# A third buffer for the odd slots' tiles, logits turned one group at a time, and a small product moved into its neighbour's PSUM pair

## The chip, the cores and the metric

The kernel runs as one program on 1 core of one Trainium2 chip. The metric is the device time of the program in microseconds, as the median of several runs. All data are 32-bit floats.

## The reference, cut to what matters

Two layers are applied to x of shape (2, 512, 32, 32). The first is an attention with deformable sampling and a learned position bias, followed by a two-matrix MLP; the second is a plain attention over the 1024 pixels. What the change touches is in the first:

```python
q = _gconv1x1(xn, qw)                        # 8 groups of 64 channels, 2 images: 16 (image, group) pairs
off = ...                                    # strided depthwise conv of q, gelu, 1x1, tanh: 64 sampled places a group
kv = _grid_sample(xn, vgrid_scaled)          # 64 sampled columns for each group
k = _gconv1x1(kv, kw); v = _gconv1x1(kv, vw)
pos = grid_q[:, :, None, :] - grid_kv[:, None, :, :]          # 1024 queries x 64 keys x 2
bias = jnp.sign(pos) * jnp.log1p(jnp.abs(pos))
bias = jax.nn.relu(bias @ cpb_w1 + cpb_b1)                    # 2 -> 128
bias = jax.nn.relu(bias @ cpb_w2 + cpb_b2)                    # 128 -> 128
bias = (bias @ cpb_w3 + cpb_b3)                               # 128 -> 1
sim = jnp.einsum('bhid,bhjd->bhij', qh, kh) + bias
attn = jax.nn.softmax(sim, axis=-1)
out = jnp.einsum('bhij,bhjd->bhid', attn, vh)
```

The bias is a small network of 128 hidden units evaluated at 16 x 1024 x 64 points. It is most of the kernel's work.

## The kernel before, in words

**The main loop** (`for s in range(NS)`, 256 slots) evaluates the bias network. There are 16 groups (image b, channel block k, half f), each with 16 slots; a slot takes 4 of the group's 64 keys and all 1024 queries. In each slot:

- `st_layer1` (L616, on VectorE, DVE): one custom instruction adds the x part and the y part of the first layer for 4 keys and clips at 0. It fills a tile h of 128 x 4096. There are 3 such tiles (tag h1), so DVE can be at most some two slots ahead of TensorE (PE).
- `st_layer2` (L633, on PE): for z = 0 to 3, eight matmuls of 128 x 32 weights by 512 columns fill a PSUM pair (two banks, 128 x 1024). Four of them work side by side on the four groups of 32 columns of the array. The pairs come from a pool `zp` of 3, which everything else that `flat(...)` asks for also draws on. ScalarE (ACT) evicts each pair with a relu: z = 0 and 2 into `rx` (3 tiles; L642), z = 1 into `ua`, `uo` or `uc` by the slot's number (L644), z = 3 into `ub` (L644). Odd slots use `uo`, of which there are 2; so a place is used again four slots later.
- `st_sum` (L652, DVE): rx and its mate are summed with weights, in place in the u tile. For z = 2 a DMA on GpSimd's queue (L654) then adds `ub` to the u tile.
- `st_fold`, `st_join`, `st_fold2`, `st_join2` (L671, L678, L687): the u tiles of eight slots are folded into one by accumulating DMAs on POOL's queue and copying DMAs on SP's queue. These read the `uo` tiles, and an eviction into `uo` has to wait for them.
- every eighth slot `st_layer3` (L719): four matmuls with the third layer's weights for each of two halves of the slots, into the group's PSUM tile `sim`, on four column groups; at the start of a pair of groups, four matmuls of q and k (L702) are put in `sim` first.

**The background.** `later()` is a generator advanced once a slot. For each channel block it makes the convolution, the offsets and the sampling; in `sample` the sampled columns kv are multiplied (L485) by the keys' weights into a pair `pkk`, of which 64 columns are used, and (L487) by the values' folded weights into a pair `pkv`, of which the first 256 columns of each bank are used. ACT then copies both out (L491, L493). kv itself comes from an addition on DVE (L478).

**The softmax.** `softmax_steps(gi)` is a generator for each group, advanced in three slots of four, one group after the other. It copies `sim` into half of a tile `ss` (L733). For f = 0 it then ends, but for the last pair. For f = 1 it transposes both halves, 8 times 128 x 128 (L744) into a pair `pt`; ACT copies it as 128 x 1024 into `sx` (L746); DVE finds the maxima (L751, L752); ACT takes exponentials (L757) and scales them (L766). At the end eight transposes (L775) write the attention back through `pb`.

**The order.** The instructions are recorded in the order of the loop; a scheduler then orders each engine's stream by what it expects to be ready, within the bounds that `issue_after` sets. So an edit in one place can move neighbours in another. [...]

**After the loop** come the output projection (L903), the MLP (L956) and the second layer (L1087, L1185), in which matrix products are made with seven block products instead of eight.

Of the kernel before, what the change touches and what calls it, by code (L numbers as in the profile page):

```python
# [8 lines left out]
F32 = mybir.dt.float32  # L9
AF = mybir.ActivationFunctionType  # L10
# [4 lines left out]
P = 128  # L15
# [3 lines left out]
DH = 64  # L19
J = 64  # L20
# [26 lines left out]
def conv_seq_kernel(ctx: ExitStack, tc: tile.TileContext, x, xt, kst, pst, cst, vec, wsm, outw, w1, w2, wl, wlt, brow, out):  # L47
    nc = tc.nc
# [6 lines left out]
    ident = cp.tile([P, P], F32, name="ident")  # L55
# [4 lines left out]
    def col(name, i=0):  # L60
        return vs[:, VOFF[name] + i : VOFF[name] + i + 1]
# [17 lines left out]
    ub = cp.tile([P, 2, NCH], F32, name="ub")  # L79
# [3 lines left out]
    kz = cp.tile([P, NCH * B, J], F32, name="kz")  # L83

    f_pool = ctx.enter_context(tc.tile_pool(name="fp", bufs=1))
    vp = f_pool.tile([P, NCH * B, C], F32, tag="vp", name="vp")
    sx = f_pool.tile([P, 8, 2, J], F32, tag="sx", name="sx")
# [47 lines left out]
    def flat(name):  # L135
        return zp.tile([P, 2, 512], F32, tag="ps2", name=name).rearrange("p h n -> p (h n)")
# [4 lines left out]
    with tc.tile_pool(name="lp", bufs=2) as lp:  # L141
# [51 lines left out]
        uo = vp[:, NCH : 2 * NCH, :]  # L193
# [221 lines left out]
        def sample(ci):  # L415
            G = CHAINS[ci]
            K = len(G)
            th = state[ci]
            gx = th[:, 0:2].rearrange("p i g j -> p (i g j)")

            nc.vector.tensor_scalar(gx, gx, 1.0, 16.0, ALU.add, ALU.mult)
            if ci > 0:
                yield


            sg = ph.tile([P, 5, 2, K * J], F32, tag="fe", name="sg")
            hat = sg[:, 0:4].rearrange("p a f j -> p (a f j)")[:, 0 : 4 * K * J]
            nc.scalar.activation(hat, gx, AF.Abs, bias=edge[:, 0:1])
            nc.scalar.activation(hat, hat, AF.Relu, bias=edge[:, 1:2])
            nc.scalar.activation(hat, hat, AF.Relu, bias=1.0, scale=-1.0)  # L430
            yield
            nc.vector.tensor_tensor(sg[:, 4], sg[:, 0], sg[:, 1], ALU.mult)
            hx = ph.tile([P, 2, K, J], F32, tag="hx", name="hx")
            hxf = hx.rearrange("p f k j -> p (f k j)")
            nc.scalar.activation(hxf, th[:, 0].rearrange("p g j -> p (g j)"), AF.Abs, bias=hb[:, 0:1])
            nc.scalar.activation(hxf, hxf, AF.Relu, bias=1.0, scale=-1.0)
            yield
            gy = th[:, 1].rearrange("p (f k) j -> p f k j", f=2)
            for i, (b, k) in enumerate(G):
                g = b * NCH + k  # L440
                xnt = ph.tile([P, 8, P], F32, name="xnt")
                nc.sync.dma_start(out=xnt, in_=xt[:, b, k])
                wk = ph.tile([P, P], F32, name="wk")
                nc.sync.dma_start(out=wk, in_=wsm[:, 512 + k * P : 512 + k * P + P])
                wt = ph.tile([P, 8, 2, J], F32, tag="xn", name="wt")
                for t in range(8):
                    if t == 4:
                        yield
                    nc.scalar.activation(wt[:, t], gy[:, :, i, :], AF.Abs, bias=hb[:, 1 + t : 2 + t])
                yield  # L450
                wtf = wt.rearrange("p t f j -> p (t f j)")
                nc.scalar.activation(wtf, wtf, AF.Relu, bias=1.0, scale=-1.0)

                kv, uv = (ph.tile([P, J], F32, name=name) for name in ("kv", "uv"))
                rowwise, natural = "p (e i t) -> p e i t", "p (i e t) -> p e i t"
                for f in range(2):
                    r, v = slice(64 * f, 64 * f + 64), sg[:, 4, f, i * J : (i + 1) * J]
                    nc.scalar.activation(
                        uv[r].rearrange(rowwise, e=2, t=16), v[r].rearrange(natural, e=2, t=16), AF.Copy,
                        scale=col("bn1b", k)[r],  # L460
                    )
                yield
                nc.vector.tensor_tensor(
                    wt, wt, hx[:, :, i, :].unsqueeze(1).to_broadcast([P, 8, 2, J]), ALU.mult
                )
                yield
                ps = flat("pkv")
                for t in range(8):
                    for f in range(2):
                        r = slice(64 * f, 64 * f + 64)  # L470
                        nc.tensor.matmul(
                            ps[r, 0:J], xnt[:, t, r], wt[:, t, f, :], start=(t == 0), stop=(t == 7)
                        )
                nc.scalar.activation(
                    kv.rearrange(rowwise, e=2, t=16), ps[:, 0:J].rearrange(natural, e=2, t=16), AF.Copy,
                    scale=bns[:, k : k + 1],
                )
                nc.vector.tensor_tensor(kv, kv, uv, ALU.add)  # L478
                if i + 1 == K and ci + 1 < len(CHAINS):
                    xn0.append(load(*CHAINS[ci + 1][0]))  # L480
                yield


                ps, pk = flat("pkv"), flat("pkk")
                nc.tensor.matmul(pk[:, 0:J], wk, kv, start=True, stop=True)  # L485
                for f_, h_, f, h in QUADS:
                    nc.tensor.matmul(  # L487
                        ps[h_, f * 512 : f * 512 + 256], kv[f_, :], uo[f_, k, h * 256 : (h + 1) * 256],
                        start=True, stop=True,
                    )  # L490
                nc.scalar.activation(kz[:, g], pk[:, 0:J], AF.Copy, scale=DH ** (-0.5))  # L491
                for f_, h_, f, h in QUADS:
                    nc.scalar.copy(vp[f_, g, h * 256 : (h + 1) * 256], ps[h_, f * 512 : f * 512 + 256])  # L493
                yield
            state[ci] = None
# [52 lines left out]
        head, g, n = chain(0), weights(0), weights(1)  # L548
# [24 lines left out]


        NS = NG * NSL
        tabs, h1s, sums, sims, logits, added = {}, {}, {}, {}, {}, {}
        evicted, raw = {}, {}


# [46 lines left out]
        def st_layer2(s):  # L626
            h1 = h1s.pop(s)
            r = []
            for z in range(4):
                ps = zp.tile([P, 2, 512], F32, name="ps2")  # L630
                for h in range(2):
                    for q in range(4):
                        nc.tensor.matmul(  # L633
                            ps[32 * q : 32 * q + 32, h, :], cw2[:, 32 * z : 32 * z + 32],
                            h1[:, 16 * h : 16 * h + 16, q, :], start=True, stop=True,
                        )
                name, bufs = (
                    ("rx", 3), (("ua", 4), ("uo", 2), ("uc", 2), ("uo", 2))[s % 4], ("rx", 3), ("ub", 3)
                )[z]
                o = lp.tile([P, 2, 512], F32, name=name, bufs=bufs)  # L640
                if z % 2 == 0:
                    nc.scalar.activation(o, ps, AF.Relu, bias=sc[:, 4 + z : 5 + z])  # L642
                else:
                    nc.scalar.activation(o, ps, AF.Relu, bias=sc[:, 4 + z : 5 + z], scale=sc[:, z : z + 1])  # L644
                r.append(o)
                if z % 2 == 1:
                    evicted.setdefault(s, []).append(nc.cur_bb.bb.instructions[-1])
            sums[s] = r
# [78 lines left out]
        def softmax_steps(gi):  # L727
            b, k, f = groups[gi]
            sim = sims.pop(gi)
            if f == 0:  # L730
                logits[0] = f_pool.tile([P, 2, 512], F32, name="ss")
            ss = logits[0]
            nc.scalar.activation(ss[:, f], sim, AF.Identity, bias=col("cb3"))  # L733
            yield

            of = [f] if gi >= NG - 2 else [0, 1][: 2 * f]
            if not of:
                return
            n = len(of)
            pt = flat("pt")  # L740
            for i, g in enumerate(of):
                for c in range(4):
                    o = 512 * i + c * P
                    nc.tensor.transpose(pt[:, o : o + P], ss[:, g, c * P : (c + 1) * P], ident)  # L744
            e = sx[:, :, of[0] : of[-1] + 1, :]
            nc.scalar.copy(  # L746
                e.rearrange("p a f j -> p f a j"), pt[:, 0 : 512 * n].rearrange("p (f a j) -> p f a j", f=n, j=J)
            )
            yield
            mx = f_pool.tile([P, 8, 2], F32, name="mx", bufs=2)  # L750
            nc.vector.tensor_reduce(mx[:, :, 0:n], e, AX.X, ALU.max)  # L751
# [20 lines left out]
            for h in range(2):  # L772
                for c in range(4):
                    n = h * 512 + c * P
# [13 lines left out]
        for s in range(NS):  # L788
# [12 lines left out]
            if s + 2 < NS:  # L801
                st_layer1(s + 2)
            st_layer2(s)


# [18 lines left out]
            if bg is None and s > ready and (s - ready) % 4 == 0 and (s - ready) // 4 <= 8:  # L824
                i = (s - ready) // 4 - 1
# [32 lines left out]
    uc = xq.tile([P, 2], F32, name="uc")  # L858
# [16 lines left out]
    with ExitStack() as top, tc.tile_pool(name="wp", bufs=2) as wp:  # L875
# [13 lines left out]
        for i, (b, h) in enumerate(halves):  # L889
            for o in range(NCH):  # L890
                n = slice(h * 512, (h + 1) * 512)
# [155 lines left out]
        for i, (b, p) in enumerate(units):  # L1047

            j, k = divmod(i, NCH)
# [323 lines left out]
```

## Time and profile before

| what | value |
|---|---|
| median of 3 runs | 2662.8 us (2661.68 to 2663.64) |
| the profiled execution: its own time | 2660.99 us |
| its span | 2659.2 us |
| PE busy | 2633.2 us, 99% |
| DVE busy | 2241.3 us, 84% |
| ACT busy | 1687.2 us, 63% |
| one h of DVE (L616) | 4.40 us |
| one eviction of ACT (L642 and L644) | 1.11 and 1.21 us |
| one sum of DVE (L652) | 1.28 us |

The main loop runs from about 37 to 1911 us. The busy time of an engine is the union of its instructions. A matmul of 512 columns leaves two records in the trace, each modelled as 0.59 us long, and four of them start together on the four column groups every 0.43 us; so "x8" in the timeline can be four matmuls of the program. In an entry of the timeline, the bracket at the end gives how long the engine had been idle and what released it. The releaser is inferred: where several things are waited for, the last to come by the profile is named, and where the engine named had long been done, it was another, often a DMA.

### The profile page before, as it was taken

The numbers are of one execution on the slowest core, as the hardware profiler recorded it, in microseconds if no ns is written. First come the engines' busy times: TensorE is split into PE (matmuls) and PEld (weight loads), VectorE is DVE, ScalarE is ACT, GpSimd is POOL, SyncE is SP. The second block draws the span as 40 slices with busy tenths as digits, with TensorE's granted clock in tenths as the row PEclk, the third lists the DMA queues.
The fourth block names the chain that finished last, engine by engine and source line by source line (L and its number), as shares of the span: only waits on it lengthen the run. The fifth ranks groups of instructions, "written<-read, shape, count | busy, mean of one in ns | idle before, by whom it ended". The sixth has DMA issues, their size and how long they took to land.

```text
span 2659.2 us, 46896 instructions
## 1 busy us (share of the span) xinstructions
PE 2633.2 (99%) x19344; PEld 965.0 (36%) x19344; DVE 2241.3 (84%) x1329; ACT 1687.2 (63%) x2201; POOL 792.3 (30%) x867
## 2 busy tenths in 40 slices
PE   9999999999999999999999999999999999999999
PEld 3332322433333333233323323333334444446454
DVE  7999999999999999999999999999674483466354
ACT  5887898789978888877777777777621131114041
POOL 1333333333333333333333333333343232000000
PEclk9999999999999999999999999999999999999999
DMA  5887878888788887888888888878730111000000
GB/s 187 181 176 169 191 164 171 181 189 180 171 176 174 192 175 172 171 177 176 171 172 183 175 178 178 172 173 181 191 110 33 48 48 48 0 16 0 32 0 32
DMA packets 116293, 366.77 MB, mean 138 GB/s; under 512 B 23376, under 2 KB 27616, under 8 KB 113392
## 3 DMA queue, kind: packets, MB, share of 16 engines
q0 software_dynamic: 69408, 235.31, 46.9%
q1 hardware_dynamic: 46240, 128.15, 13.8%
q8 instruction: 153, 2.51, 0.4%
q14 instruction: 60, 0.49, 0.1%
q10 hardware_dynamic: 432, 0.31, 0.0%
HBM read 74.81 MB, written 6.55 MB: 31 GB/s over the span
## 4 chain that ended last, share of the span: by engine, by line
PE 60%; DMA 25%; DVE 7%; issue 6%; ACT 1%; POOL 1%; SPq 0%; POOLq 0%; DVEq 0%; ACTq 0%
PE ps L633 31%; PE sw L956 14%; PE sw L1087 9%; DMA uc<-uo 7%; DMA uc<-uc 6%; DMA ua<-uc 4%; DMA uc<-ub 4%; DVE h L616 3%; PE sw L1185 2%; DMA ua<-uo 1%; DVE ub L652 1%; PE psg L535 1%; DMA ua<-ua 1%; PE sim L719 1%; DVE uo L652 1%
## 5 line engine op out<-in xcount | busy, mean ns | idle before, releaser
L633 PE MATMUL ps<-h,cw 128*32 128x512 f32 x16384 | 1782.8, 592 | 8.1 <-ACT rx L642 6.1
L616 DVE CUSTOM_DVE_ANT_1 h<-ta,tb 128x4096 f32<-128x4096 f32 (+1 forms) x257 | 1131.0, 4402 | 28.1 <-PE ps L633 24.2
L633 PEld LDWEIGHTS ps<-h,cw 128*32 128x32 f32 x16384 | 554.7, 110 | 1205.0 <-issue 1114.6
L642 ACT ACTIVATE rx<-ps,sc 128x1024 f32<-128x1024 f32 x512 | 568.1, 1110 | 146.3 <-PE ps L633 116.4
L644 ACT ACTIVATE ub<-ps,sc 128x1024 f32<-128x1024 f32 x256 | 308.2, 1204 | 80.5 <-PE ps L633 80.2
L652 DVE SCALAR_TENSOR_TENSOR ub<-rx,sc,ub 128x1024 f32<-128x1024 f32 x256 | 326.8, 1277 | 6.6 <-ACT ub L644 6.6
L671 POOL DMA_DIRECT2D ua<-uc x126 | 158.3, 1272 | 299.5 <-DMA ua<-uc 292.5
L671 POOL DMA_DIRECT2D ua<-ua x189 | 225.4, 1336 | 20.2 <-DMA ua<-uo 16.2
L644 ACT ACTIVATE uo<-ps,sc 128x1024 f32<-128x1024 f32 x128 | 154.2, 1205 | 74.3 <-PE ps L633 46.2
L956 PE MATMUL sw<-xb,w1t 128*128 128x512 f32 x448 | 193.7, 592 | 2.7 <-DVE xs L123 2.7
L956 PE MATMUL sw<-hm,w2t 128*128 128x512 f32 x448 | 193.6, 592 | 0.0
L654 POOL DMA_DIRECT2D uo<-ub x127 | 126.8, 998 | 210.8 <-DVE ub L652 200.1
L652 DVE SCALAR_TENSOR_TENSOR uo<-rx,sc,uo 128x1024 f32<-128x1024 f32 x128 | 163.5, 1278 | 18.9 <-ACT uo L644 18.9
L123 DVE TENSOR_TENSOR hm<-hm,sw 128x1024 f32<-128x1024 f32 x56 | 67.6, 1218 | 104.5 <-PE sw L956 104.3
L671 POOL DMA_DIRECT2D uc<-uo x63 | 54.0, 857 | 340.8 <-DMA uc<-uo 340.4
L956 PEld LDWEIGHTS sw<-xb,w1t 128*128 128x128 f32 x448 | 85.0, 190 | 110.2 <-issue 105.7
L965 ACT ACTIVATE hm<-hm,vs 128x512 f32<-128x512 f32 x64 | 42.6, 713 | 128.4 <-DVE hm L123 128.4
L956 PEld LDWEIGHTS sw<-hm,w2t 128*128 128x128 f32 x448 | 85.1, 190 | 107.1 <-issue 106.2
L123 DVE TENSOR_TENSOR xs<-xs,sw 128x1024 f32<-128x1024 f32 (+1 forms) x48 | 55.6, 1171 | 75.9 <-PE sw L1087 36.0
L654 POOL DMA_DIRECT2D ua<-ub x64 | 59.3, 926 | 178.4 <-DVE ub L652 163.4
L1087 PE MATMUL sw<-aT,vt 128*128 128x512 f32 x224 | 96.7, 593 | 0.3 <-ACT aT L1167 0.3
L596 ACT ACTIVATE ta<-fb,vs 128x512 f32<-128x512 f32 (+1 forms) x65 | 88.5, 1364 | 10.1 <-DMA fb<-fdr 10.1
(247 smaller groups left out, 2191.6 us busy)
## 6 DMA issues: line engine op xcount, KB each, us to landing
uo<-ub POOLq DMA_DIRECT2D x127, 512.0 KB, 5.5
fb<-fdr SPq DMA_DIRECT2D x64, 512.0 KB, 5.2
ua<-ub POOLq DMA_DIRECT2D x64, 512.0 KB, 6.0
uc<-ub POOLq DMA_DIRECT2D x64, 512.0 KB, 5.0
ua<-ua POOLq DMA_DIRECT2D x63, 256.0 KB, 6.3
ua<-uo SPq DMA_DIRECT2D x63, 256.0 KB, 2.5
ua<-uo POOLq DMA_DIRECT2D x63, 256.0 KB, 5.6
uc<-uc POOLq DMA_DIRECT2D x63, 256.0 KB, 7.2
```

The costliest lines, as they stand in the source:

```text
L123: nc.vector.tensor_tensor(out, a, b_, op)
L596: nc.scalar.activation(ta.rearrange("p j x -> p x j")[:, :, j0:j1], fb[:, 0, :, j0:j1], AF.Identity, bias=col("cb1"), scale=col("w1x"),)
L616: nc.vector._custom_dve(TENSOR_ADD_SAT, out=h1[:, y : y + step].rearrange("p y t x -> p (y t x)"), in0=a.unsqueeze(1).to_broadcast([P, ste ...
L633: nc.tensor.matmul(ps[32 * q : 32 * q + 32, h, :], cw2[:, 32 * z : 32 * z + 32], h1[:, 16 * h : 16 * h + 16, q, :], start=True, stop=True,)
L642: nc.scalar.activation(o, ps, AF.Relu, bias=sc[:, 4 + z : 5 + z])
L644: nc.scalar.activation(o, ps, AF.Relu, bias=sc[:, 4 + z : 5 + z], scale=sc[:, z : z + 1])
L652: nc.vector.scalar_tensor_tensor(r[1], r[0], sc[:, z : z + 1], r[1], ALU.mult, ALU.add)
L654: nc.gpsimd.dma_start(out=sums[s][1], in_=sums[s][3], accum_op=ALU.add)
L671: nc.gpsimd.dma_start(out=out, in_=in_, accum_op=ALU.add)
L956: nc.tensor.matmul(ps[:, m, :], w[:, a, k, m * P : (m + 1) * P], x[:, b_, k, :], start=(k == 0), stop=(k == 1),)
L1087: nc.tensor.matmul(ps[:, m, :], w[:, a, k, c + m * P : c + (m + 1) * P], x[b_][:, k, :], start=(k == 0), stop=(k == nk - 1),)
L1185: nc.tensor.matmul(v[:, m, :], xbl[b_][:, k, m * P : (m + 1) * P], gn[:, a, k, :], start=(k == 0), stop=(k == 1),)
```

## The change

Three edits, in one diff:

- `uo` has 3 places instead of 2; a place is used again six slots later.
- `ss` is one tile of 128 x 512 for each group in turn. Each group is transposed in its own step, 4 times 128 x 128 into the first half of a pair `pt`, and ACT copies 128 x 512 into that group's half of `sx`. The rest of the softmax still runs once for both groups of a pair.
- the keys' product goes into columns 256 to 319 of the first bank of the pair that the values' product also uses; `pkk` is gone.

```diff
-                ps, pk = flat("pkv"), flat("pkk")
-                nc.tensor.matmul(pk[:, 0:J], wk, kv, start=True, stop=True)
+                ps = flat("pkv")
+                pk = ps[:, 256 : 256 + J]
+                nc.tensor.matmul(pk, wk, kv, start=True, stop=True)
                 for f_, h_, f, h in QUADS:
...
-                nc.scalar.activation(kz[:, g], pk[:, 0:J], AF.Copy, scale=DH ** (-0.5))
+                nc.scalar.activation(kz[:, g], pk, AF.Copy, scale=DH ** (-0.5))
...
                 name, bufs = (
-                    ("rx", 3), (("ua", 4), ("uo", 2), ("uc", 2), ("uo", 2))[s % 4], ("rx", 3), ("ub", 3)
+                    ("rx", 3), (("ua", 4), ("uo", 3), ("uc", 2), ("uo", 3))[s % 4], ("rx", 3), ("ub", 3)
                 )[z]
...
             sim = sims.pop(gi)
-            if f == 0:
-                logits[0] = f_pool.tile([P, 2, 512], F32, name="ss")
-            ss = logits[0]
-            nc.scalar.activation(ss[:, f], sim, AF.Identity, bias=col("cb3"))
+
+            ss = f_pool.tile([P, 512], F32, name="ss")
+            nc.scalar.activation(ss, sim, AF.Identity, bias=col("cb3"))
             yield
-
+            pt = flat("pt")[:, 0:512]
+            for c in range(4):
+                nc.tensor.transpose(pt[:, c * P : (c + 1) * P], ss[:, c * P : (c + 1) * P], ident)
+            nc.scalar.copy(sx[:, :, f, :], pt.rearrange("p (a j) -> p a j", j=J))
             of = [f] if gi >= NG - 2 else [0, 1][: 2 * f]
             if not of:
                 return
             n = len(of)
-            pt = flat("pt")
-            for i, g in enumerate(of):
-                for c in range(4):
-                    o = 512 * i + c * P
-                    nc.tensor.transpose(pt[:, o : o + P], ss[:, g, c * P : (c + 1) * P], ident)
             e = sx[:, :, of[0] : of[-1] + 1, :]
-            nc.scalar.copy(
-                e.rearrange("p a f j -> p f a j"), pt[:, 0 : 512 * n].rearrange("p (f a j) -> p f a j", f=n, j=J)
-            )
             yield
```

More of the change, by code (lines that the diff above doesn't have):

```diff
@@ L575, in conv_seq_kernel @@
         NS = NG * NSL
-        tabs, h1s, sums, sims, logits, added = {}, {}, {}, {}, {}, {}
+        tabs, h1s, sums, sims, added = {}, {}, {}, {}, {}
         evicted, raw = {}, {}
```

## The prediction, written before the changed kernel was run

> **What bounds the kernel now.** I read the page first, then the table by stages, then the waits, then the timeline of TensorE around each place that the diff touches.
>
> From the page:
> ```profile
> PE 2633.2 (99%) x19344; PEld 965.0 (36%) x19344; DVE 2241.3 (84%) x1329; ACT 1687.2 (63%) x2201; POOL 792.3 (30%) x867
> L633 PE MATMUL ps<-h,cw 128*32 128x512 f32 x16384 | 1782.8, 592 | 8.1 <-ACT rx L642 6.1
> ```
> TensorE is busy 99% of the span: whatever doesn't change its matmul stream or its stalls is worth nothing. The stages (columns: length, then busy time of PE, PEld, DVE, ACT, POOL):
> ```profile
> 620.00:880.00 260.00, 257.33 (x2432) 81.41 (x2424) 259.70 (x139) 223.00 (x316) 93.56 (x108) 1.00 0.80 174
> 921.00:1148.00 227.00, 223.54 (x2098) 68.59 (x2094) 226.23 (x122) 193.37 (x268) 80.93 (x93) 1.00 0.82 175
> 1148.00:1860.00 712.00, 711.46 (x6610) 229.14 (x6606) 690.11 (x318) 540.17 (x636) 260.20 (x299) 1.00 0.82 176
> ```
> The first two rows have DVE at 99.9% and 99.7% while PE stalls: there DVE sets the pace, and PE time saved inside becomes waiting. In the third PE is never idle, so each extra matmul counts. At 541 to 620 and 880 to 921 the timeline shows DVE's h (L616) waiting for PE with its three h tiles full: PE sets the pace.
>
> The waits (us, times, longest), of PE and then of ACT:
> ```profile
> PE ps L633 <- ACT rx L642: 6.1, 11, 1.1
> PE ps L633 <- ACT uo L644: 1.6, 2, 1.5
> ...
> ACT uo L644 <- DMA ua<-uo: 11.8, 8, 2.1
> ACT uo L644 <- DMA uc<-uo: 10.9, 8, 2.9
> ```
> ACT often stands before the eviction into uo until the DMAs that read its old contents are done (22.7 us), but little of it reaches PE. The timeline gives the cases in which it does:
> ```profile
> 256.97 1.21 ACT L644 ACTIVATE uo<-ps,sc 128x1024 f32<-128x1024 f32 x1 [2.88 <-PE ps L633]
> 258.23 2.35 PE L633 MATMUL ps<-h,cw 128*32 128x512 f32 x20 [1.46 <-ACT uo L644]
> ```
> ACT is idle 2.88 us with PE's pair long written; PE, its three pairs full, stops for 1.46 us. The profile names PE as releaser, but PE had gone on and finished: it is the buffer.
>
> The matmuls of the logits (sim), and the transposes:
> ```profile
> 112.33 0.62 PE L719 MATMUL sim<-ua,w3f 128*32 128x512 f32 x1
> 112.78 0.62 PE L633 MATMUL ps<-h,cw 128*32 128x512 f32 x2
> 112.78 0.59 PE L719 MATMUL sim<-ua,w3f 128*32 128x512 f32 x1
> 112.79 14.32 PE L633 MATMUL ps<-h,cw 128*32 128x512 f32 x126
> 127.04 1.09 PE L273 MATMUL psq<-xn,wq 64*64 64x512 f32 x8
> ...
> 1018.94 1.04 PE L719 MATMUL sim<-ua,w3f 128*32 128x512 f32 x8
> 1019.80 0.61 PE L633 MATMUL ps<-h,cw 128*32 128x512 f32 x4
> ```
> ```profile
> 1270.85 1.09 PE L744 MATMUL pt<-ident,ss 128*128 128x128 f32 x8
> 1271.87 2.35 PE L633 MATMUL ps<-h,cw 128*32 128x512 f32 x20
> ...
> 1868.66 0.66 PE L744 MATMUL pt<-ident,ss 128*128 128x128 f32 x4
> 1869.25 2.34 PE L633 MATMUL ps<-h,cw 128*32 128x512 f32 x18
> ```
> [...] Four sim matmuls on the four column groups cost 1019.80 - 1018.94 = 0.86 us together; a single one, behind the keys' product, also keeps its group for 0.86 us.
>
> [...] four records of L633 start together every 0.43 us, and a change of form costs about 0.12 us. [...] ACT stood idle 2.88 us with nothing passed ahead. [...] the small product's eviction (kz) now waits for the last matmul of the pair. [...] the trace has 577 and 1003 for the copies out of pt.
>
> **The change part by part.** The order in which the built program issues the instructions shows, beside the edits, one thing that the diff doesn't: seven times a sim matmul stood alone after the keys' product (six from ua, one from qa), three followed later; now all four stand together at the later place. POOL and SP keep their order; DVE swaps a few neighbours.
>
> 1. Third uo place. It removes waits of at most 2.9 us, one use further back (two slots, some 14 us) being ample. PE stalls that end with it (idle + 0.16, since a record is modelled 0.59 long and the pitch is 0.43): 256: 1.46 + 0.16 = 1.6; 523: 0.66 + 0.16 less 0.1 for the change of form = 0.7; 1816: two gaps, 0.6. Sum -2.9. The other uo waits (815, 831 and so on) lie where DVE paces or PE had full pairs: nothing. Bounds 0 (the stall moves to rx) and -4.
>
> 2. Logits' matmuls together. From 112.33 to 127.04 are 14.71 us; 128 records of L633 need 32 x 0.43 = 13.74 and the change of form 0.12: the lone matmul cost 0.85. Its three mates cost 0.65 at 135 (7.75 us from 128.06 to 135.81, of which 66 records are 16.5 x 0.43 = 7.09). 0.85 + 0.65 - 0.86 = 0.64 saved, at 111, 293, 578, 1183, where a full-width operation between the two makes all groups wait for the laggard: -2.6. At 532 nothing full-width stands between, total excess 2.27 against 1.91 without a split: -0.35. At 834 no loss can be found: 0. The qa one at 880: 0.95 + 1.01 - 0.97, less some drain: -0.9. Sum -3.85, bounds -2 and -5.
>
> 3. Keys' product in the pair's free columns. The matmuls stay. Only one pair is taken: at 579 pkv waited 0.30 for a second pair, in a stretch where PE paces: -0.3. The longer stalls at pkk (1.1 at 835.94, 1.59 at 1138.43) look like this too ("ACT rx"), but kv<-kv,uv (DVE L478) ran 835.63 to 835.84 behind an h: they wait for kv and stay. kz waits for the quads now, 0.66 us later, but the four copies behind it had waited for them anyway: 0.
>
> 4. Transposes by group. Seven pairs: one batch of eight becomes two of four. From the fence: 1271.87 - 1270.85 = 1.02 and 0.59, with 0.12 on entry 1.14 and 0.71: a further batch +0.71, the smaller old one -0.43. The new batches stand near 205, 503, 737, 976, 1213, 1440, 1666, the old near 325, 562, 796, 1033, 1270, 1497, 1724. Those of 737, 796, 976, 1033 lie where DVE paces: 0. The rest: 5 x 0.71 - 5 x 0.43 = +1.4. ACT gets a copy of 0.58 and gives back 0.43: 0.15 seven times, in idle time; without that cover 1. A new batch takes a pair in the rotation; the tile behind it waits for ACT's copy if ACT is behind: 0 to 1.1 each, I take 0. DVE's max (mx) comes after DVE's h in places; Exp starts about 10 us after mx in the trace, more than the 4.4 of an h: 0.
>
> Sum: -2.9 - 3.85 - 0.3 + 1.4 = -5.65. The profiled execution took 2660.99 us around its span of 2659.2: 2655.3 for it. It lies 1.8 under the median of the runs, so for the median 2662.8 - 5.6 = 2657.2.
>
> **The rivals.**
> *More than that* (0.12): the stalls of the DVE-paced stretches shrink too, because ACT no longer blocks: at 418.5 a uo wait of 1.15 stood ahead of the late gelu (gof). Against it: DVE has no idle time there to give. -9 to -11: 2652.5.
> *Only one of the two* (0.18): either the uo stalls move to rx, whose evictions waited 16.6 us for DVE's ub, leaving -2.8 (2660.0), or the matmuls' laggard was hidden, leaving -1.8 (2661.0).
> *Slower* (0.10): the new batches collide with ACT. At 345 to 354 and 820 PE stalls because ACT is behind (a table load, prod). If each of seven new batches holds its pair for an eviction of 1.1 us, 7 x (0.28 + 1.1) = +9.7, less half of the gains, 2.8: +6.9, 2669.7. It decides from four such places. Against it: ACT is 63% busy, and the old batches led to 1.8 us of weight-load waits over 6 times, hidden mostly.
>
> **How the numbers follow.** The likeliest case (0.60) has its own range of 2654 to 2660.5; its centre is just past the bound of 0.2% (5.3 us, about what a measurement of this kernel can tell from no change; 2657.5), so I give 0.42 of it to faster, 0.18 to the same. With 0.12 faster from the first rival, 0.18 same from the second, and of the slow one 0.02 same, 0.08 slower: 0.54, 0.38, 0.08. The range 2652 to 2663.5 leaves out the slow case and half of the fast one.
>
> **What would show it.** Right: no wait of "ACT uo" for a DMA; PE without the stalls at 256, 523 and 1816; no sim x1 behind pkv, sim x8 everywhere; pt x4 with 0.71 us a batch; the stalls at pkv's small product still there, for kv. Wrong: "PE ps <- ACT sx" behind pt, "rx <- DVE ub" grown by what uo lost, or stretches 620 to 880 and 921 to 1148 that became shorter.

## The result, and the profile after

| | before | after |
|---|---|---|
| median | 2661.96 us (2658.98 to 2665.62, 20 runs) | 2657.51 us (2654.91 to 2662.28, 20 runs) |
| ratio to before | | 0.9986, 95% interval 0.9979 to 0.9992 |
| profiled execution: time, span | 2660.99, 2659.2 us | 2662.28, 2660.4 us |
| last transposes into pb in the loop | 1846.90 us | 1841.74 us |
| first matmul of the output projection | 1908.38 us | 1906.96 us |
| first matmul of the MLP | 1966.10 us | 1965.56 us |

The changed kernel is faster by 0.14%: 3.7 us by the ratio (interval 2.1 to 5.6), 4.4 us by the medians. The forecast was 2657.2. The execution that was profiled is the slowest of its 20, so the two spans stand the wrong way round: the trace has to be read stage by stage. Lines of the changed kernel have numbers one higher than before up to the softmax, and five lower after it (L633 is now L634, L719 L720, L744 L737, L903 L898, L956 L951).

The page's row of the bias network's matmuls:
```profile
L634 PE MATMUL ps<-h,cw 128*32 128x512 f32 x16384 | 1778.4, 592 | 5.4 <-ACT rx L643 4.2
```
The idle time ahead of L634 fell from 8.1 to 5.4 us. The stages, with the columns as before (length; busy PE, PEld, DVE, ACT, POOL; granted clock, DMA share, GB/s), and two short windows near the end:
```profile
620.00:880.00 260.00, 257.31 (x2433) 79.62 (x2428) 259.40 (x138) 222.43 (x312) 92.99 (x107) 1.00 0.82 178
921.00:1148.00 227.00, 224.13 (x2101) 68.75 (x2097) 226.07 (x123) 193.53 (x271) 80.56 (x93) 1.00 0.80 174
1148.00:1860.00 712.00, 711.71 (x6606) 238.51 (x6602) 689.99 (x319) 539.62 (x633) 260.39 (x300) 1.00 0.82 175
1904.40:1907.80 3.40, 3.40 (x11) 0.80 (x6) 0.00 (x0) 0.00 (x0) 0.00 (x0) 0.50 0.00 0
1965.90:1969.30 3.40, 3.40 (x5) 1.33 (x4) 0.00 (x0) 0.00 (x0) 0.42 (x1) 0.50 0.95 366
```
In the first two rows DVE still sets the pace (99.8% and 99.6%), with PE idle for 2.7 and 2.9 us (before 2.7 and 3.5). The last two rows are new: TensorE's granted clock is 0.50 there; in the kernel before it was 1.00 over the same stretches.

The waits of PE that changed:
```profile
PE ps L634 <- ACT rx L643: 4.2, 8, 1.2
...
PE sim L720 <- DMA uc<-ub: 2.7, 1, 2.7
PE pkv L486 <- ACT rx L643: 1.7, 1, 1.7
...
PE pkv L486 <- ACT ub L645: 1.5, 1, 1.5
```
No wait of "ACT uo" for a DMA is left, and none of PE for "ACT uo". The two long waits ahead of the keys' product are still there, now named pkv (1.7 and 1.5 us, before 1.6 and 1.1). And a wait of 2.7 us for a DMA, which was 0.17, has appeared.

The logits' matmuls and the transposes (TensorE's timeline):
```profile
112.63 13.94 PE L634 MATMUL ps<-h,cw 128*32 128x512 f32 x128
126.50 1.09 PE L273 MATMUL psq<-xn,wq 64*64 64x512 f32 x8
...
134.41 1.04 PE L720 MATMUL sim<-ua,w3f 128*32 128x512 f32 x8
...
206.88 0.66 PE L737 MATMUL pt<-ident,ss 128*128 128x128 f32 x4
207.47 1.06 PE L634 MATMUL ps<-h,cw 128*32 128x512 f32 x8
```
From 112.63 to 126.50 are 13.87 us, exactly 32 x 0.43 and 0.11 for the change of form: the lone matmul that used to make this 14.71 (with itself) is gone, and all four stand at 134.41. A batch of four transposes lasts 0.59 before the next L634.

So in this execution the loop did what was forecast: the last transposes into pb came 5.16 us earlier, 5.5 counted from the first matmuls of L634 in the loop (37.55 against 37.22). Then most of it was lost. The end of the loop, before and after:
```profile
1904.47 1.03 PE L719 MATMUL sim<-ua,w3u 128*32 128x512 f32 x4
1905.33 1.03 PE L719 MATMUL sim<-uo,w3u 128*32 128x512 f32 x4
1906.54 0.62 PE L719 MATMUL sim<-uc,w3u 128*32 128x512 f32 x2 [0.17 <-DMA uc<-ub]
...
1908.38 1.98 PE L903 MATMUL sw<-qa,vp 128*128 128x512 f32 x4
```
```profile
1899.31 1.03 PE L720 MATMUL sim<-ua,w3u 128*32 128x512 f32 x4
1900.17 1.03 PE L720 MATMUL sim<-uo,w3u 128*32 128x512 f32 x4
1903.89 0.62 PE L720 MATMUL sim<-uc,w3u 128*32 128x512 f32 x2 [2.68 <-DMA uc<-ub]
...
1905.05 1.98 PE L720 MATMUL sim<-uo,w3u 128*32 128x512 f32 x4
1906.96 2.40 PE L898 MATMUL sw<-qa,vp 128*128 128x512 f32 x4
```
From the first of these matmuls to the projection: 3.91 us before, 7.65 after, so 3.74 of 5.16 given back; 2.51 of that is the longer wait (2.68 - 0.17), the rest falls into the stretch right behind it, where the granted clock was 0.50 from 1904.42 on, for 3.41 us (the same four records took 1.98 instead of 1.05). Why the DMA was late is in POOL's timeline, before and after:
```profile
1901.03 0.83 POOL L671 DMA_DIRECT2D ua<-uc  x1 [5.48 <-DMA ua<-uc]
1901.57 1.19 POOL L654 DMA_DIRECT2D uc<-ub  x1
```
```profile
1898.08 0.83 POOL L672 DMA_DIRECT2D ua<-uc  x1 [5.70 <-DMA ua<-uc]
1898.61 1.19 POOL L655 DMA_DIRECT2D uc<-ub  x1
```
In both traces POOL issues uc<-ub right behind a fold (0.54 and 0.53 us later), and it had stood 5.48 and 5.70 us before that fold, until the fold before it had landed. PE arrived 5.16 us earlier, this DMA was issued only 2.96 us earlier. The MLP's first matmul waits for DVE, too (3.09 us, before 2.74), and the granted clock was 0.50 a second time, from 1965.86 for 3.41 us: the MLP's first 56 records took 26.00 us, before 24.30. The kernel was 0.54 ahead at that point and ends 1.2 behind.

### The profile page after: what moved, and what is told of

Read it like the earlier page. It is cut to its first block, busy times and chain, and to the rows that moved or that the text cites. A ratio compares the mean times of both kernels' runs of the same rounds, so it can differ in the third digit from the quotient of the medians.

```text
span 2660.4 us, 46899 instructions
## 1 busy us (share of the span) xinstructions
PE 2634.7 (99%) x19344; PEld 961.9 (36%) x19344; DVE 2242.7 (84%) x1329; ACT 1689.0 (63%) x2208; POOL 790.7 (30%) x867
## 3 DMA queue, kind: packets, MB, share of 16 engines
q8 instruction: 153, 2.51, 0.4%
## 4 chain that ended last, share of the span: by engine, by line
PE 80%; DVE 7%; DMA 6%; issue 5%; ACT 2%; POOL 0%; DVEq 0%; SPq 0%; POOLq 0%; ACTq 0%
PE ps L634 50%; PE sw L951 15%; PE sw L1082 9%; DVE h L617 2%; DMA uc<-uo 2%; PE sw L1180 2%; DMA ua<-uc 1%; DMA uc<-uc 1%; DVE ub L653 1%; PE psg L536 1%; PE sim L720 1%; DMA uc<-ub 1%; DVE uo L653 1%; PE sw L898 1%; ACT rx L643 0%
## 5 line engine op out<-in xcount | busy, mean ns | idle before, releaser
L634 PE MATMUL ps<-h,cw 128*32 128x512 f32 x16384 | 1778.4, 592 | 5.4 <-ACT rx L643 4.2
L634 PEld LDWEIGHTS ps<-h,cw 128*32 128x32 f32 x16384 | 550.3, 110 | 1197.9 <-issue 1125.3
L951 PE MATMUL sw<-xb,w1t 128*128 128x512 f32 x448 | 195.4, 596 | 3.1 <-DVE xs L123 3.1
L951 PE MATMUL sw<-hm,w2t 128*128 128x512 f32 x448 | 193.6, 592 | 0.0
L951 PEld LDWEIGHTS sw<-xb,w1t 128*128 128x128 f32 x448 | 85.6, 191 | 111.7 <-issue 106.8
L951 PEld LDWEIGHTS sw<-hm,w2t 128*128 128x128 f32 x448 | 85.1, 190 | 107.1 <-issue 106.2
L985 ACT COPY hm<-sw 128x1024 f32<-128x1024 f32 x8 | 8.1, 1009 | 136.6 <-PE sw L951 136.6
```

What stands on the lines that cost most here:

```text
L634: nc.tensor.matmul(ps[32 * q : 32 * q + 32, h, :], cw2[:, 32 * z : 32 * z + 32], h1[:, 16 * h : 16 * h + 16, q, :], start=True, stop=True,)
L951: nc.tensor.matmul(ps[:, m, :], w[:, a, k, m * P : (m + 1) * P], x[:, b_, k, :], start=(k == 0), stop=(k == 1),)
```

## The experiments

Every experiment was timed against the kernel before on the same chip. Differences in microseconds are the ratio's distance from 1 times 2662; the intervals reach 1.7 to 2.5 us to either side. "Last pb" is the start of the last transposes into pb inside the loop (1846.90 in the kernel before).

**The product alone.** The kernel before with the third edit only:
```diff
-                ps, pk = flat("pkv"), flat("pkk")
+                ps = flat("pkv")
+                pk = ps[:, 256 : 256 + J]
```


> The kernel before with the third edit alone (the keys' product in the free columns of the values' pair). In the built program this alone puts six of the seven lone logits' matmuls together again. My theory: the split of four matmuls into one and three cost 3.85 us in the loop and the second pair 0.3, so the last transposes back to qa (pb) start 4.1 us earlier than in the kernel before (at 1842.2 instead of 1846.4), and the median falls by 2 to 4 us, the rest going to a wait at the loop's end. Rival: the gain of this edit is the freed pair alone, 0.3 us, and the order of the four matmuls is hidden: pb at 1846, the median unchanged.

Measured: 2657.01 us, ratio 0.9986 (0.9979 to 0.9992), as good as the whole change. Its last pb stands at 1839.09, 7.8 us earlier than before where 4.1 were expected; the profiled execution is the fastest of its 21. It also brings the logits' matmuls together, and with two places of uo it has no stall of PE for uo, though ACT waits longer for uo's readers than before (18.4 and 23.3 us against 11.8 and 10.9):
```profile
ACT uo L645 <- DMA uc<-uo: 23.3, 16, 2.6
ACT uo L645 <- DMA ua<-uo: 18.4, 12, 2.7
```
No stall of PE follows from them in this execution. So the stalls for uo are no fixed property of two places.

**The transposes alone.** The kernel before with the second edit only.

> The kernel before with the second edit alone (each group's logits turned in its own step, four transposes instead of eight). My theory: a further batch costs 0.71 us, the old ones save 0.43, four of the fourteen lie where DVE sets the pace: +1.4 us at the last pb (1847.8), the median up by 1 to 2 us. Rival: the new batches hold a PSUM pair while ACT is behind, 1.1 us each: +7 us. A third: the extra batches are hidden, 0.

Measured: 2666.48 us, ratio 1.0022 (1.0012 to 1.0031): slower by 5.9 us, where 1.4 were forecast. The loop itself lost 3.84 (last pb at 1850.74). ACT's and PE's timelines at the worst place:
```profile
818.97 1.20 ACT L644 ACTIVATE uo<-ps,sc 128x1024 f32<-128x1024 f32 x1 [3.49 <-DMA ua<-uo]
```
```profile
820.23 1.92 PE L633 MATMUL ps<-h,cw 128*32 128x512 f32 x16 [2.74 <-ACT uo L644]
823.31 1.07 PE L633 MATMUL ps<-h,cw 128*32 128x512 f32 x8 [1.16 <-ACT rx L642]
```
ACT stands 3.49 us before an eviction into uo, and PE runs out of pairs for 2.74 us, in a stretch where DVE paces; from the pb near 709 to the one near 948 it took 241.27 us, before 238.58. More uo stalls follow at 1116, 1494, 1793 and 1807 (0.67, 0.97, 0.24, 0.46), while those of the kernel before at 256 and 523 are absent, with the same two places. The added work is small; the waits that it meets are not. Why the readers of uo are late at these places isn't shown.

**Third place and transposes.**

> The kernel before with the third place for uo and the logits turned by group (the third place alone has no room in SBUF; the smaller ss makes it). The logits' matmuls stay split and the keys' product keeps its own pair. My theory: -2.9 + 1.4 = -1.5 us at the last pb (1844.9), no stall of TensorE at 256, 523 and 1816, no wait of ACT's uo evictions for a DMA; the median falls by 0 to 1.5. Rival: the stalls move to the evictions into rx: +1.4 as without the third place, pb at 1847.8.

Measured: 2662.91 us, ratio 1.0009 (1.0002 to 1.0015). No stall of PE for uo is left, and 3.5 us of the 5.9 are back. The logits still stand apart (one, then three): it is the product's edit that brings them together.

**The third place alone.** The kernel before with three places of uo; the batch of eight stays, and since a tile ss of two halves doesn't fit beside the third place, the first group's logits wait in half of sx:
```diff
-                    ("rx", 3), (("ua", 4), ("uo", 2), ("uc", 2), ("uo", 2))[s % 4], ("rx", 3), ("ub", 3)
+                    ("rx", 3), (("ua", 4), ("uo", 3), ("uc", 2), ("uo", 3))[s % 4], ("rx", 3), ("ub", 3)
...
+            early = sx.rearrange("p a f j -> p (a f j)")[:, 0:512]
+            ss = f_pool.tile([P, 512], F32, name="ss") if of else early
```


> The kernel before with a third place for uo and nothing else: pkk keeps its own pair, the eight transposes of a pair of groups stay in one batch (the first group's logits wait in half of sx, since a tile ss of two halves no longer fits beside the third place). Theory, the first step of the prediction: TensorE's stalls at 256, 523 and 1816 go, -2.9 us, 2658.8, ratio 0.9989, with the last transposes into pb near 1844 instead of 1846.9. Rival (the stalls move to rx or come and go with the phase of the DMAs; the product alone had none of them with two places): the kernel before, 2661.5, ratio 1.0.

Measured: 2660.86 us, ratio 0.9998 (0.9990 to 1.0006): no change that can be measured; -2.9 lies just outside the interval. Yet the last pb of its trace stands at 1843.87, where 1844 was expected. The 3.0 us are made of other parts than the forecast's: between the first pb and the second 0.84 (0.7 were forecast, for 523); ahead of the last pb 2.0, of which 0.6 were forecast (a wait for a fold at 1767, shown further down, is absent here as well); and ahead of the first pb, where 1.6 were forecast, only 0.2. They are lost again behind the loop: the last slots' logits wait 1.60 us for uc<-ub (before 0.17), and the MLP's first 56 records take 26.00 us instead of 24.30, as in after, where 3.41 us of them ran at 0.50. Near the first uo stall PE's and ACT's timelines now show
```profile
252.94 7.50 PE L633 MATMUL ps<-h,cw 128*32 128x512 f32 x68 [1.69 <-ACT rx L642]
```
```profile
250.06 1.35 ACT L596 ACTIVATE ta<-fb,vs 128x512 f32<-128x512 f32 x1 [2.27 <-DMA fb<-fdr]
```
In place of the stall for uo there is one of 1.69 us for rx, three pairs of L633 earlier: ACT had stood 2.27 us before another instruction (ta, L596), whose DMA landed at 250.06. It stood there in the kernel before as well (1.99, until 248.53), and in the whole change for 0.30 (until 247.01). In these three traces the wait at this place ends with that DMA.

**Product and transposes, uo at two places.**

> The changed kernel with uo at two places again (the keys' product in the pair and the transposes by group stay; the order of instructions is the same as in the changed kernel). Theory: the third place is worth what separates the run with the transposes alone from the one with the third place beside them, 3.4 us, because the earlier copies of the transposes make ACT late for an eviction into uo whose readers are late too: 2661, ratio 0.9997 against the kernel before, with PE stalled near 817 behind a wait of ACT uo for a DMA. Rival (with the logits together TensorE's stream is shifted and the uo waits fall where three full pairs cover them, as in the run with the product alone, which had no such stall): no change from the changed kernel, 2657.5, ratio 0.9986.

Measured: 2659.88 us, ratio 0.9996 (0.9988 to 1.0004), near what the theory said, and the uo stall near 817 is there:
```profile
815.37 1.92 PE L634 MATMUL ps<-h,cw 128*32 128x512 f32 x16 [1.06 <-ACT uo L645]
```
It is 1.06 us here, not 2.74. The interval touches that of the whole change, so the third place's 2.7 us beside the other two are likely, not certain. The order of the instructions is that of the whole change.

**Product and third place, transposes in one batch.** The changed kernel with eight transposes in a batch again, the first group's logits kept in half of sx as above:

> The changed kernel with the eight transposes of a pair of groups in one batch again: the first group's logits are put into the first half of sx, which is idle then, so that ss stays at 128 x 512 and uo keeps its third place. My theory: the seven further batches are undone, -1.4 us at the last pb against the changed kernel (1841.2 to 1839.8), the median 0 to 1.5 lower. Rival: what the batches cost was hidden: no difference.

Measured: 2656.46 us, ratio 0.9984 (0.9975 to 0.9994). Its last pb stands at 1837.51, where 1839.8 was expected. Counted from the first matmuls of L634 it comes 4.1 us before that of after, but only 1.4 and 1.7 before those of two more executions of the same loop (shown below): the forecast price of the batches, 1.4, fits these two.

With these, the eight combinations of the three edits are complete (us against the kernel before, 2662 x (ratio - 1)):

| edit | alone | beside uo | beside the product | beside the transposes | beside both others |
|---|---|---|---|---|---|
| third uo place | -0.5 | | -0.5 | -3.5 | -2.7 |
| product in the pair | -3.7 | -3.7 | | -6.9 | -6.1 |
| transposes by group | +5.9 | +2.9 | +2.7 | | +0.5 |

A difference of two ratios is good to some 2.4 to 3.3 us (an estimate from the intervals). The product carries the change. The third place shows a gain beside the transposes alone (-3.5), and just fails to be clear of the error beside both others. That the transposes cost least where the other two have given room is what the last row looks like; its steps from 2.9 to 0.5 are within the error.

**Logits split on purpose.** The changed kernel with 31 of the logits' groups split again into one matmul and, a slot later, the rest, in most places with nothing of full width between them (full width: an operation that takes all four column groups at once):
```diff
+                            if e == h == m == 0 and s + 8 < NS:
+                                yield
...
-                st_layer3(s - 12)
+                rest = st_layer3(s - 12)
+                next(rest)
```


> The changed kernel with one of the four logits' matmuls of each eighth slot issued in its slot and the other three behind the next slot's matmuls: 31 splits instead of none (the order elsewhere stays). Nothing full-width stands between the one and the three in most places. My theory: a split costs what it cost at 532 in the kernel before, 0.35 us, in the 22 or so places where TensorE sets the pace: +8 us against the changed kernel. Rival: without a full-width operation between them the laggard is caught up, a split costs 0 to 0.05 us: at most +1 us.

Measured: 2659.74 us, ratio 0.9994 (0.9986 to 1.0002), 2.1 us above the changed kernel with intervals that overlap: far from 8 us more. TensorE's timeline:
```profile
134.26 0.59 PE L720 MATMUL sim<-ua,w3f 128*32 128x512 f32 x1
134.26 0.63 PE L634 MATMUL ps<-h,cw 128*32 128x512 f32 x3
134.69 0.59 PE L720 MATMUL sim<-ua,w3f 128*32 128x512 f32 x1
134.72 5.76 PE L634 MATMUL ps<-h,cw 128*32 128x512 f32 x51
```
At 134.26 the lone matmul starts beside three of L634: the other column groups go on, and later the three mates let this one catch up. The stretch around it, from psq at 126.35 to the offsets' matmuls (po) at 190.19, is only 0.02 us longer than in another execution of the changed kernel (63.84 against 63.82). Two splits did cost: right behind the matmuls of q and k at 191 and 427 the stretch to the next full-width operation is 0.68 and 0.62 us longer (16.43 against 15.75, 43.89 against 43.27), although only L634 stands between the parts. Three groups start late there while the fourth goes on, so that PE counts as busy; what they wait for isn't shown. Counted from the loop's first matmuls to the last pb but one, the splits cost 1.4 to 2.2 us against three executions of the changed loop. So the split itself is cheap, and what made it dear in the kernel before is most likely the full-width operation between its parts (psq or pb); no run puts one there on purpose.

**The last slot by matmul.** The changed kernel with the last DMA uc<-ub taken out of the loop; the logits' matmuls take that tile by itself, four more of them:
```diff
-            if z == 2 and s < NS - 1:
+            if z == 2 and s < NS - 2:
...
-                parts[1].append((w[3], sums[s + 7][3]))
-                parts[0] = 4 * [None] + parts[0]
+                parts[1] += [(w[2], sums[s + 6][3]), (w[3], sums[s + 7][3])]
+                parts[0] = 5 * [None] + parts[0]
```


> The changed kernel with the last accumulating DMA of the loop left out (slot 254, ub onto uc) and its part added by two more matmuls into the logits, as slot 255 has it already; the result is the same. My theory: at the loop's end TensorE waited 2.7 us for this DMA and then ran at half clock for 3.4 us, so that 4 us of the loop's gain were given back in the profiled execution: now no such wait, pt of the last group 2.5 us earlier relative to the last pb, and 1.7 us more where the half clock had followed; the median falls by 2 to 4 us. Rival: the next matmuls of the logits wait for DVE's last sums anyway: at most 0.5 us.

Measured: 2655.95 us, ratio 0.9977 (0.9969 to 0.9985). The end of the loop in its timeline:
```profile
1896.51 1.03 PE L720 MATMUL sim<-ua,w3u 128*32 128x512 f32 x4
...
1900.90 1.99 PE L898 MATMUL sw<-qa,vp 128*128 128x512 f32 x4
```
4.39 us to the projection instead of 7.65, and each four records of the logits take 1.03 us: the DMA's wait was the cause of that loss. The granted clock was 0.50 from 1933.6 to 1936.9 instead. Against the changed kernel the ratio falls by 2.4 us, with intervals that overlap.

**Fillers ahead of the MLP.** The changed kernel with six matmuls of no use to the result before the MLP, to keep TensorE busy:
```diff
+        idle = flat("idle")
+        for _ in range(6):
+            nc.tensor.matmul(idle[:, 0:512], op1[0][0][:, 0, 0:P], op1[1][0][:, 0, :], start=True, stop=True)
```


> The changed kernel with six matmuls of 512 columns, whose result is not used, issued after the output projection, where TensorE waits about 3 us for DVE before the MLP. My theory: they fill 2.6 us of that wait, so that TensorE's clock is not halved after it; -1.7 us in the executions in which it was, none in the others; the median 0.5 to 1.7 us lower, the spread smaller. Rival: the clock doesn't depend on this wait: no difference, or up to +0.3 us where the fillers end late.

Measured: 2659.53 us, ratio 0.9993 (0.9985 to 1.0001): no gain. The timeline ahead of the MLP:
```profile
1959.68 5.31 PE L1038 MATMUL idle<-qa,vp 128*128 128x512 f32 x12
1960.93 1.22 DVE L123 TENSOR_TENSOR xs<-xs,sw 128x1024 f32<-128x1024 f32 x1
1965.06 24.30 PE L951 MATMUL sw<-xb,w1t 128*128 128x512 f32 x56
```
The six fillers leave twelve records and take 5.3 us, twice the 2.6 that were expected. DVE's addition, for which the MLP waits in the changed kernel, ends at 1962.15, and the MLP starts at 1965.06: the fillers delay what they should prepare by some 2.9 us. The granted clock was 0.50 from 1900.9 to 1904.2 here, and eight records of the projection, at 1937.28, took 5.40 us, where they took 3.70 in after (at 1940.37).

This kernel is the same as the changed one up to there (POOL's next eight instructions from 1750.08 in after and from 1746.36 in this one stand in the same order), so it shows what two executions of one program differ by: its last pb stands at 1838.73, 3.0 us earlier. TensorE's timeline at the logits of one group, after, then this one:
```profile
1761.89 1.02 PE L720 MATMUL sim<-ua,w3f 128*32 128x512 f32 x2
1763.20 0.63 PE L720 MATMUL sim<-ua,w3f 128*32 128x512 f32 x3 [0.29 <-DMA ua<-uc]
```
```profile
1760.21 1.04 PE L720 MATMUL sim<-ua,w3f 128*32 128x512 f32 x8
```
In the profiled execution of after, three of the four matmuls wait for the folding DMA; from here to the next group's start are 57.24 us against 55.91, and the stretch before it took 0.91 more. POOL's timeline shows where the folds fall behind, after and then this one:
```profile
1750.08 0.85 POOL L672 DMA_DIRECT2D uc<-uo  x1 [8.09 <-DMA uc<-uo]
```
```profile
1746.36 0.85 POOL L672 DMA_DIRECT2D uc<-uo  x1 [6.35 <-DMA uc<-uo]
```
The same fold was waited for 8.09 us in one execution and 6.35 in the other. The last slot by matmul has this loop, too, but for its last DMA, and lies between: 56.52 us to the next group. The kernel before had such a wait at 1767.74, too (0.34; 57.90 to the next group, some 1.4 beyond what the uo stall at 1816 explains).

**All three of these together** (one batch, the last slot by matmul, the fillers).

> The changed kernel with the transposes in one batch, the last slot's part added by matmuls, and the fillers before the MLP. My theory: the three add up, -1.4 - 3 - 1 = -5.4 us against the changed kernel, 10 us or 0.37% under the kernel before. Rival: the loop's end keeps what the batches give (the DMAs of the last slots end when they end), -3 us.

Measured: 2657.09 us, ratio 0.9980 (0.9972 to 0.9987): not the sum; the fillers gave nothing alone, either. Eight records of the projection, at 1933.85, took 6.76 us, where they took 3.70 in after.

**The same without the fillers, and the smallest version.**

> The changed kernel with two edits, without the fillers: the eight transposes of a pair of groups in one batch again, and the last slots' tiles multiplied on TensorE instead of being added by a DMA. Theory: a batch saves what half batches cost (some 1 us), the end saves the wait of 2.7 us before the last logits, and the two add because they lie in different places: 2654.5, ratio 0.997 against the kernel before. Rival (the ends only move where TensorE's clock is halved for 3.4 us, and the loop varies by 3 us from execution to execution): no more than either alone, 2656, ratio 0.998.

Measured: 2654.72 us, ratio 0.9976 (0.9966 to 0.9985), the fastest kernel of the study by its median.

The product in the pair and the last slot by matmul, put into the kernel before with nothing else:

> The kernel before with the keys' product in the pair and with the last slots' tiles multiplied on TensorE instead of added by a DMA; two places of uo and eight transposes in one batch stay. Theory: the product's edit alone gave 0.9986; the end takes away the wait before the last logits, and no other edit of the three is needed: 2655, ratio 0.9975. Rival (what the end saves comes back as a halved clock or as a wait further on): 2657, ratio 0.9986 as the product alone.

Measured: 2656.01 us, ratio 0.9978 (0.9968 to 0.9987). Two small edits do as well as any other kernel here; what the batch and the third place add to them can't be told apart from nothing. Up to the loop's end this is the program of the product alone, and here PE does stall for uo, at 1109, 1484 and 1783 (0.60, 0.47 and 0.41 us), where it had no such stall:
```profile
1484.16 7.07 PE L634 MATMUL ps<-h,cw 128*32 128x512 f32 x64 [0.47 <-ACT uo L645]
```
The last slot by matmul gives 2.4 us beside the whole change, 2.1 beside product and third place, and 2.1 beside the product alone. Each is within its error; the three together are 2.2, give or take 1.8 (an estimate from their intervals).

## Why the prediction was right, and where its steps were not

The time, 2657.2 against 2657.51, and the likeliest case held. The sum of -5.65 was made for the loop of the profiled execution, and there it was -5.5; against the ratio it is 2 us too large (-3.7, interval -5.6 to -2.1). Part of the agreement is luck. The -5.5 belongs to one execution: the two others of the same loop (last slot by matmul, fillers) come to -7.9 and -8.2 against the same trace of before. The profiled execution of after lost 2.2 us in the waits for folds near 1704 and 1762, for which the forecast had no term, and that of before some 1.4. And at the projection's first matmul, counted from the first of the loop, 1.8 us are left of the gain in after and 3.8 in the run with the fillers.

1. *Third uo place, -2.9.* The three stalls are gone in the trace of after, and ACT's 22.7 us of waiting for uo's readers with them. But alone the edit gave -0.5: near 256 a stall stood behind rx, which was the rival's "move to rx", and what its loop gained in the trace (3.0 us) was lost behind the loop. The stalls at 256 and 523 are absent from all four other traces with two places of uo, which in part stall elsewhere. The step failed in taking the stalls of one execution as owed to the number of places. What the third place is worth seems to depend on how late ACT is: -3.5 and -2.7 beside the transposes by group.

2. *Logits together, -3.85.* Right in kind: it comes with the product's edit, and it saves where a full-width operation stood between (the 14.71 us at 111 became 13.87 without the lone matmul). The small products, the full-width operation and the logits near 111, 293 and 1183 took some 3.6 us each beyond the pitch of L634 (0.43 us from one set of four records to the next) before and 2.8 to 3.0 after: -0.63, -0.63 and -0.75 against the forecast 0.64. At 578 it is -0.45, beside the 0.30 of step 3. The one of q and k at 880: from the keys' product to psq 15.67 us before, 14.83 after (875.87 to 890.70), so -0.84 against 0.9. At 532 from the keys' product to the end of the logits 2.14 beyond the pitch before, 1.82 after: -0.3, as forecast, though most of the splits made on purpose between L634's own matmuls cost far less.

3. *Keys' product, -0.3.* The long stalls ahead of it stayed for kv, as said: the addition into kv ends at 831.42 and 1132.77, and the product starts at 831.53 and 1132.87. The wait of 0.30 at 579 is gone; it stands (0.24 to 0.31) in all three runs that keep the pair pkk. With step 2 the edit measures -3.7 alone where -4.15 were forecast for both.

4. *Transposes, +1.4.* The prices were right (0.59 for a batch of four, with the change of form 0.7). With the third place beside it, the last pb stands at 1845.19 (transposes by group) and at 1843.87 (batch of eight): +1.3, with one execution each. But alone the edit cost +5.9. The step put the cost of a later ACT at 0, and named the pair behind it as what could wait; what did wait was the eviction into uo, for 3.49 us. The forecast's slow rival was this sort of collision with another place: it is real without the third uo place, and no trace shows it with it.

5. *Not foreseen: the end of the loop.* The prediction ended its sum at the loop. Behind it the logits of the last slots wait for POOL's last DMA, 2.68 us instead of 0.17, and in after the granted clock was 0.50 for 3.41 us. The last slot by matmul shows the size of it: 4.39 us instead of 7.65 on that stretch. That the wait is long wherever the transposes are by group (2.3 to 3.2 us in the six traces that have both them and this DMA) and shorter elsewhere (0.17 to 1.60 in four) is seen; why is open.

The ratio's missing 2 us are about what the last slot by matmul gives back (2.2, give or take 1.8), so the wait for POOL's last DMA can account for them. The stretches at a granted clock of 0.50 hardly can. The trace of before happens to have none between 1900 and 1975 us and that of after two of 3.41 us each, but over all executions the granted clock averages 0.9989 in both kernels (20 of after, and the 140 of before that were timed beside the experiments; each is recorded to three digits).

## What to carry to other kernels

Follow a saving past the stage in which it arises, to the next transfer that isn't moved with it: the queue of chained DMAs was moved by 3 us where the matmuls were moved by 5. A stall behind a buffer can be one execution's own (those at 256 and 523 stand in one of the five traces with two places of uo), so try the edits alone and in pairs before giving each a price. And where the parts of a packed matmul stand apart, look first for something of full width between them: with it the parts cost 0.6 to 0.8 us more here, among the loop's own matmuls mostly next to nothing (0.02 at 134, 0.6 to 0.7 at 191 and 427).

## What the runs showed of the hardware

*The clock.* In the trace of after TensorE's granted clock was 0.50 for 3.41 us from 1904.42 and again for 3.41 us from 1965.86: 0.53 us after the end of a wait of 2.68 us, and 0.30 us after the end of one of 3.09. In the trace of before it was 1.00 from 4.91 to 2657.07, behind waits of 2.76 us (until 1941.37) and 2.74 (until 1966.10) as well. The MLP's first 56 records took 26.00 us in after and 24.30 in before, a difference of 1.70. The timelines of the experiments have both values, and the wait of PE ahead of the MLP is no guide to which: 26.00 behind 2.17 us (one batch and the last slot by matmul), 2.69 (third place alone), 2.85 (product and third place) and 3.02 (third place and transposes), 24.30 behind 2.43 (product alone), 2.60 (last slot by matmul), 2.87 (product and transposes) and 3.01 (logits split). What else has to come together isn't shown here. Eight records of the projection, behind another wait for DVE (2.66 and 3.04 us), took 6.76 and 6.74 us in two runs (all three together; product and last slot), and 3.70 in before and after (behind 2.76 and 2.75).

*Column groups.* In the run with the split logits one lone matmul on one group (two records, 0.43 us apart) didn't hold up the other three: at 134.26 three records of L634 start beside it, and the stretch around it was 0.02 us longer. At 191 and 427 such a split cost 0.68 and 0.62 us all the same. With the full-width psq behind it, in the kernel before, it was 14.71 us from the lone matmul to psq; without the lone matmul, in after, 13.87.

*DMA folds.* The same accumulating DMA was waited for 6.35 and 8.09 us in two executions of the same program up to that point; PE took 55.91 and 57.24 us from the logits there to the next group, and 56.52 in the run with the last slot by matmul, which differs by its last DMA.
